# Cross attention, causal attention and eight experts on one core: the experts' step on routed tokens, in slots of 32

## The chip, the cores and the metric

The kernel runs on one core of a Trainium2 chip. The metric is the device time of one execution in microseconds. Three runs of the kernel before gave 585.03, 585.13 and 585.42, median 585.13. The profile shows the instructions of five engines: TensorE (PE, with its weight loads as PEld), VectorE (DVE), ScalarE (ACT), GpSimd (POOL) and SyncE (SP), whose queue issues all DMAs here.

## The reference

The state `x` has 256 tokens of 512 features. Three steps are added to it in turn.

- Cross attention without softmax over a context of 25088 rows: `sigmoid(q k^T / sqrt(128)) v`, with q from the normalized state, and k and v from the context.
- Causal attention with 16 heads of 32 features, low-rank keys and values, a rotary part, and an output projection.
- Eight experts, one for each token, chosen by the largest gate logit:

```
logits = einsum('th,eh->te', xf, gate_w)
onehot = one_hot(argmax(logits), 8)
g = einsum('th,ehd->etd', xf, wg);  u = einsum('th,ehd->etd', xf, wu)
inter  = square(relu(g)) * u * onehot.T[:, :, None]
out    = einsum('etd,edh->th', inter, wd)
```

As written, every expert is computed for every token, and the one-hot vector then clears all but one. An expert has 512 x 128 weights twice (g and u) and 128 x 512 once.

## The kernel before, in words

**Tiles.** The 256 tokens are two tiles of 128 (`tt` or `t`, 0 and 1). The 512 features are four blocks of 128 (`j`, KD = 4). The context is read in 49 chunks of 512 rows.

**Precision.** Where it matters, an f32 operand is split into a high part, rounded by ACT (line 64), and a low part, subtracted on DVE (line 65). `mm3` (lines 67 to 70) then makes three fast matmuls of them (hi x hi, hi x lo, lo x hi) on operands of the type `fp32r`. Other products are plain f32 matmuls, which TensorE runs as two records.

**The loop** (lines 263 to 294). For each chunk: projected keys (`kp_mm`), scores and sigmoid (`scores`), and the product with the context into two PSUM banks, `acc[0]` and `acc[1]`, one for each token tile (`av`, line 192). The products of tile 1 for the last two chunks are put off into the list `late` (eight calls, `AV1`). `prepare` (line 198) takes one piece of a list `todo` per chunk: it loads 128 x 512 weights, splits them and, except for `wv`, stores both halves to DRAM (`spill`). The list has 32 pieces: 4 of `wv`, 16 of `gu` (g and u), 8 of `dn` (down) and 4 of `wo`.

**Behind the loop** (lines 298 to 711) each step is a small function, and the calls at the bottom are its order. `O1`, `O2` and `V` apply the value projection to `acc`. `N1` adds and normalizes: residual add, two steps of moments and a sum on DVE, a power on POOL (line 129), the scaling on DVE (line 134). `X` transposes. `QR`, `CKV`, `KR`, `K`, `VS` and `Q` make queries, keys and values, `S` the scores and exponentials, `PT` their transpose, and `PV` the product with the values: line 457 writes 32 PSUM partitions for each head, so it uses 32 columns of the array. `R1`, `R2` and `AT` divide by the sums, `WO` projects, `N2` normalizes again, `Y` transposes and splits, and `LG` (line 500) takes the logits and writes the one-hot matrix `hot`.

**The experts before.** `GU` multiplies all 128 tokens of a tile by g and u of two experts (512 columns, `mm3`, four blocks: 12 matmuls per pair and tile; the last pair of tile 1 is done expert by expert with 256 columns). `GE` forms relu(g) squared times u times the column of `hot`. `IT` transposes and splits it, `DN` multiplies by the down weights, all experts into one bank `fo`, and `OUT` adds the residual and stores. `load_gu` and `load_dn` fetch the split weights from DRAM behind the loop. `GU` of tile 0 begins while the attention of tile 1 still runs.

**The order.** `in_order` (line 35) ties each instruction of PE, ACT, DVE and POOL to the one before it on its engine, so each engine runs in program order; SP takes its issues in turn. A buffer is named by its tag; with `bufs=2` a new tile waits until all readers of the tile two before it are done. PSUM banks come from one ring of six (`bank`).

Of the kernel before, what the change touches and what calls it, by code (L numbers as in the profile page):

```python
# [20 lines left out]
P = 128  # L21
# [9 lines left out]
LAG = 2  # L31
MASKED = -3.0e38

# [15 lines left out]
def body(ctx, tc, a, out, nch=NCH):  # L49
# [55 lines left out]
    spill = {n: dram.tile([P, 2 * w], F32, name=f"sp_{n}") for n, w in (("wo", KD * D), ("gu", E * 2 * D), ("dn", E * D))}  # L105

    todo = [("wv", at, None, at) for at in range(0, KD * D, D)]
    todo += [("gu", at, 4 * D, at // (4 * D) * 8 * D + at % (4 * D)) for at in range(0, E * 2 * D, D)]
    todo += [("dn", at, D, 2 * at) for at in range(0, E * D, D)]
# [9 lines left out]
    iota8 = sm.tile([P, E], F32, name="iota8")  # L119
    nc.gpsimd.iota(iota8, pattern=[[1, E]], base=-E, channel_multiplier=0, allow_small_or_imprecise_dtypes=True)  # L120
# [176 lines left out]

    x1 = [sb.tile([P, D], F32, name=f"x1{t}") for t in range(2)]
    x2 = [None, None]
# [3 lines left out]
    xn = [None, None]  # L303
# [7 lines left out]

    gu, dn = [None] * E, [None] * E

    def load_gu(e, tag, bufs):
        gu[e] = sb.tile([P, 2, 2 * D], F32R, tag=tag, name=f"gu{e}", bufs=bufs)
        nc.sync.dma_start(f(gu[e]), spill["gu"][:, e * 4 * D:(e + 1) * 4 * D].rearrange("p (i w) -> p i w", i=2))

    def load_dn(e, tag, bufs):
        dn[e] = pair(f"dn{e}", [P, D], tag, bufs)
        for i in range(2):  # L320
            nc.sync.dma_start(f(dn[e][i]), spill["dn"][:, (2 * e + i) * D:(2 * e + i + 1) * D])

    for e, (tag, bufs) in enumerate((("T0", 2), ("T0", 2), ("T1", 1), ("rN", 2), ("rN", 2))):
        load_gu(e, tag, bufs)
    for e, (tag, bufs) in enumerate((("w", 2), ("w", 2), ("kp", 2), ("dn", 1))):
        load_dn(e, tag, bufs)
    trig = sb.tile([64, T], F32, tag="qp0", name="trig")
    nc.sync.dma_start(trig, a["trig"])
    vs = [sb.tile([P, D], F32, tag=f"kp{i}", name=f"vs{i}", bufs=2) for i in range(2)]

    def O1(tt):
        o = tmp(f"o{tt}")
        copy(o, acc[tt])
        return o

    def O2(tt, o):
        split(oh[:, :, toks(tt)], ol[:, :, toks(tt)], transposed(bank(f"o_ps{tt}"), o))

    def V(tt):
        ps = bank(f"v_ps{tt}")  # L340
        for j in range(KD):
            w = slice(j * D, (j + 1) * D)
            mm3(ps, oh[:, j, toks(tt)], ol[:, j, toks(tt)], wv[0][:, w], wv[1][:, w], j == 0, j == KD - 1)
        return ps

    def N1(tt, ps):
        tt2(x1[tt], ps, x_sb[tt], ALU.add)
        xn[tt] = normal(x1[tt], moments(x1[tt], f"b{tt}"), f"xb{tt}")

    def X(tt):  # L350
        copy(xT[tt], transposed(bank(f"xb_ps{tt}"), xn[tt]))
# [12 lines left out]
    ckv, qr = [None] * 2, [None] * 2  # L364

    def CKV(tt):
        ps = bank(f"ckv_ps{tt}")[:, 0:P]
        prod(ps, tt, lambda j: pw["wkvd"][:, toks(j)])
        ckv[tt] = sb.tile([P, P], F32, name=f"ckv{tt}")
        copy(ckv[tt], ps)  # L370

    def QR(tt):
        ps = bank(f"qr_ps{tt}")[0:64, 0:P]
        prod(ps, tt, lambda j: pw["wqr"][:, 64 * j:64 * (j + 1)])
        qr[tt] = sb.tile([32, P], F32, name=f"qr{tt}")
        rotated("q", qr[tt], ps, tt)
        for i, r in enumerate((64, 0)):
            nc.vector.tensor_scalar(qs[r:r + 32, tt, i], qr[tt][:, None, :].broadcast_to([32, KD, P]), 0.125, None, ALU.mult)

    def KR(tt):  # L380
        ps = bank(f"kr_ps{tt}")[0:64, 0:P]
        mm(ps, lhsT=pw["wkr"], rhs=ckv[tt], start=True, stop=True)
        kr = sb.tile([32, P], F32, tag="kr", name=f"kr{tt}")
        rotated("k", kr, ps, tt)
        for r in (64, 0):
            for h in range(2):
                (vcopy if h else copy)(kbd[h][r:r + 32, :, 2 - r // 32:4 - r // 32, toks(tt)],
                                       kr[:, None, None, :].broadcast_to([32, 2, 2, P]))

    def K(tt):  # L390
        for h in range(2):
            ps = bank(f"k_ps{tt}{h}")[:, :2 * P].rearrange("p (g t) -> p g t", g=2)
            for g in range(2):
                mm(ps[:, g, :], lhsT=pw["wku"][:, toks(2 * h + g)], rhs=ckv[tt], start=True, stop=True)
            for j in range(4):
                r = slice(32 * j, 32 * j + 32)
                (vcopy if h else copy)(kbd[h][r, :, j, toks(tt)], ps[r])

    def VS(tt):
        ps = bank(f"vs_ps{tt}")  # L400
        mm(ps, lhsT=ckv[tt], rhs=pw["wvu"], start=True, stop=True)
        copy(vs[tt], ps)

    qps = [None, None]

    def Q(tt, g):
        if g == 0:
            qps[tt] = bank(f"q_ps{tt}").rearrange("p (g t) -> p g t", g=KD)
        prod(qps[tt][:, g, :], tt, lambda j: pw["wq2"][:, j * D + g * P:j * D + (g + 1) * P])
        if g == KD - 1:  # L410
            for i in range(2):
                r = slice(64 * i, 64 * i + 64)
                nc.scalar.activation(qs[r, tt, i], qps[tt][r], AF.Copy, scale=0.125)
# [3 lines left out]
    pr, pt = {}, {}  # L417
# [4 lines left out]
    def S(tt, u):  # L422
        g, h0, n = heads(tt, u)
        nk = P * (tt + 1)
        p3 = bank(f"s{tt}_{u}").rearrange("p (h k) -> p h k", h=n)
# [7 lines left out]
        mx = sm.tile([P, 4], F32, tag="mx", name=f"mx{tt}_{u}", bufs=4)  # L433
        nc.vector.tensor_reduce(mx[:, :n], p3, AX.X, ALU.max, negate=True)
        pr[tt, u] = sb.tile([P, D], F32, tag="wr", name=f"pr{tt}_{u}", bufs=2).rearrange("p (h k) -> p h k", h=n)
        for i in range(n):
            h = 4 * g + h0 + i
            nc.scalar.activation(pr[tt, u][:, i, :], p3[:, i, :], AF.Exp, bias=mx[:, i:i + 1],
                                 accum_out=sums[:, tt, h:h + 1])

    def PT(tt, u):
        n = heads(tt, u)[2]
        ps = bank(f"pt{tt}_{u}")
        for i in range(n):
            for kt in range(tt + 1):
                nc.tensor.transpose(ps[:, toks(i * (tt + 1) + kt)], pr[tt, u][:, i, toks(kt)], ident)  # L446
        pt[tt, u] = sb.tile([P, D], F32, tag="z", name=f"pt{tt}_{u}", bufs=2)
        vcopy(pt[tt, u], ps)

    def PV(tt, u):  # L450
        g, h0, n = heads(tt, u)
        if u == 0:
            pv[tt] = psum.tile([P, KD, P], F32, tag=f"acc{tt}", name=f"pv{tt}")
        for i in range(n):
            r = slice(32 * (h0 + i), 32 * (h0 + i + 1))
            for kt in range(tt + 1):
                mm(pv[tt][r, g, :], lhsT=vs[kt][:, g * P + r.start:g * P + r.stop],  # L457
                   rhs=pt[tt, u][:, toks(i * (tt + 1) + kt)], start=kt == 0, stop=kt == tt)

    rT2, att = [None] * 2, [None] * 2  # L460

    def R1(tt):
# [6 lines left out]
    def R2(tt):  # L469
        ps = transposed(bank(f"r_ps{tt}"), rT2[tt])  # L470
        rT2[tt] = tmp(f"rT{tt}").rearrange("p (g t) -> p g t", g=KD)
        copy(rT2[tt], ps)

    def AT(tt):
        at = tmp(f"at{tt}").rearrange("p (g t) -> p g t", g=KD)
        tt2(at, pv[tt], rT2[tt], ALU.mult)
        att[tt] = [t.rearrange("p (g t) -> p g t", g=KD) for t in pair(f"at{tt}", [P, D], "at")]
        split(*att[tt], at)

    def WO(tt):  # L480
        ps = bank(f"wo_ps{tt}")
        for g in range(KD):
            w = slice(g * D, (g + 1) * D)
            mm3(ps, att[tt][0][:, g, :], att[tt][1][:, g, :], wo[0][:, w], wo[1][:, w], g == 0, g == KD - 1)
        x2[tt] = sb.tile([P, D], F32, tag=f"x{tt}", name=f"x2{tt}")
        tt2(x2[tt], ps, x1[tt], ALU.add)
        xn[tt] = moments(x2[tt], f"c{tt}")

    def N2(tt):
        xn[tt] = normal(x2[tt], xn[tt], f"xc{tt}")  # L490

    def Y(tt):
        ps = transposed(bank(f"xc_ps{tt}"), xn[tt])
        split(yhl[0][:, :, toks(tt)], yhl[1][:, :, toks(tt)], ps)
        yT[tt] = sb.tile([P, KD, P], F32, tag=f"xT{tt}", name=f"yT{tt}")
        copy(yT[tt], ps)

    hot = [None, None]

    def LG(tt):  # L500

        ps = bank(f"lg_ps{tt}")[:, 0:E]
        for j in range(KD):
            mm(ps, lhsT=yT[tt][:, j, :], rhs=pw["gate"][:, j * E:(j + 1) * E], start=j == 0, stop=j == KD - 1)
        lg = sm.tile([P, E], F32, tag="lg", name=f"lg{tt}")
        m1 = sm.tile([P, 1], F32, tag="m1", name=f"m1{tt}")
        vcopy(lg, ps)
        nc.vector.tensor_reduce(m1, lg, AX.X, ALU.max)
        nc.vector.scalar_tensor_tensor(lg, lg, m1, iota8, ALU.is_ge, ALU.mult)
        nc.vector.tensor_reduce(m1, lg, AX.X, ALU.min)  # L510
        hot[tt] = sm.tile([P, E], F32, name=f"hot{tt}")
# [261 lines left out]
```

## Time and profile before

| what | value |
|---|---|
| median of three runs | 585.13 us |
| profiled execution, own time | 584.47 us |
| its span | 582.7 us |
| TensorE busy | 568.9 us, 98% |
| DVE, ACT, POOL busy | 459.9, 395.1, 21.2 us |
| loop's last matmul of `acc[0]` begins | 480.26 us |
| WO(1) ends, first transpose of IT begins | 548.03 us |
| last matmul begins | 578.63 us |
| granted TensorE clock | 1.00 |

A busy TensorE is a modelled figure, since matmuls overlap: a matmul of 512 columns has a duration of about 0.39 us, while the next begins 0.23 us later. So the starts of neighbours count, not the durations. A line number in a row can be that of a helper (lines 64, 65 and 68 to 70 serve many steps); the names of the tiles tell them apart.

### The profile page before, as it was taken

Reading aid. Unit: us, or ns where it says so; the run is one execution under the profiler, and the core shown is the slowest. Engines: PE = TensorE matmul, PEld = TensorE weight load, DVE = VectorE, ACT = ScalarE, POOL = GpSimd, SP = SyncE. Lnnn points to the kernel's source line nnn. Section 1 sums busy time; section 2 is a strip of 40 time slices with the busy share of each in tenths; the row PEclk is TensorE's granted clock in tenths of the full one; section 3 lists DMA queues with packets and bytes.
Section 4 is the critical chain, followed back from the end, with each engine's and each line's share of the span. In section 5 each row is a group of like instructions: output and inputs, shape, how many; then the busy total and the mean of one; then the engine's idle time right before and its main releaser. Section 6 shows DMA issues by size and latency. Waiting matters only on the chain.

```text
span 582.7 us, 7892 instructions
## 1 busy us (share of the span) xinstructions
PE 568.9 (98%) x2952; PEld 476.3 (82%) x2952; DVE 459.9 (79%) x528; ACT 395.1 (68%) x512; POOL 21.2 (4%) x28
## 2 busy tenths in 40 slices
PE   4999999999999999999999999999999998999997
PEld 3888888888888888888888888888888887876886
DVE  6998888888888888888888888787878765667543
ACT  5887777777777777777777776767676753565221
POOL 5200000000000000000000000000000041000000
PEclk9999999999999999999999999999999999999999
DMA  8998787888887888788988897565656477800000
GB/s 293 360 350 299 272 302 271 328 278 321 278 331 269 328 266 336 265 332 288 342 285 307 282 338 242 213 224 209 227 206 232 156 294 260 325 2 1 1 0 38
DMA packets 33527, 144.94 MB, mean 249 GB/s; under 512 B 4241, under 2 KB 4433, under 8 KB 19793
## 3 DMA queue, kind: packets, MB, share of 16 engines
q1 hardware_dynamic: 33488, 144.44, 69.2%
q8 instruction: 23, 0.38, 0.2%
q14 instruction: 16, 0.12, 0.1%
HBM read 129.22 MB, written 15.20 MB: 248 GB/s over the span
## 4 chain that ended last, share of the span: by engine, by line
PE 94%; DVE 3%; DMA 1%; issue 0%; POOL 0%; ACT 0%; SPq 0%; POOLq 0%
PE acc L68 15%; PE acc L69 15%; PE acc L70 15%; PE kp_ps L68 8%; PE kp_ps L69 8%; PE kp_ps L70 8%; PE sc L70 4%; PE sc L69 4%; PE sc L68 4%; PE s L429 2%; PE gu L68 1%; PE gu L70 1%; PE gu L69 1%; PE pt L446 1%; DMA wq_r<-in_wq 1%; PE pv L457 1%
## 5 line engine op out<-in xcount | busy, mean ns | idle before, releaser
L68 PE MATMUL acc<-N,z 128*128 128x512 f32 x392 | 153.9, 393 | 0.0
L69 PE MATMUL acc<-N,z 128*128 128x512 f32 x392 | 153.7, 392 | 0.0
L65 DVE TENSOR_TENSOR N<-rN,N 128x2048 fp32r<-128x2048 f32 (+1 forms) x53 | 112.1, 2119 | 52.2 <-ACT N L64 52.2
L70 PE MATMUL acc<-N,z 128*128 128x512 f32 x392 | 152.5, 389 | 0.0
L65 DVE TENSOR_TENSOR T<-rT,T 128x2048 fp32r<-128x2048 f32 (+1 forms) x49 | 110.2, 2250 | 15.1 <-ACT T L64 15.1
L187 ACT ACTIVATE z<-sc 128x512 f32<-128x512 f32 x98 | 58.7, 599 | 66.4 <-PE sc L70 66.2
L64 ACT CAST N<-rN 128x2048 fp32r<-128x2048 f32 (+1 forms) x55 | 94.4, 1725 | 6.1
L64 ACT CAST T<-rT 128x2048 fp32r<-128x2048 f32 (+1 forms) x55 | 94.4, 1721 | 1.6 <-DMA rT<-in_ctxT 1.5
L70 PEld LDWEIGHTS acc<-N,z 128*128 128x128 f32 x392 | 73.6, 188 | 16.1
L68 PEld LDWEIGHTS acc<-N,z 128*128 128x128 f32 x392 | 74.0, 189 | 12.3
L69 PEld LDWEIGHTS acc<-N,z 128*128 128x128 f32 x392 | 74.0, 189 | 11.6
L68 PE MATMUL kp_ps<-T,wk 128*128 128x512 f32 x196 | 76.9, 392 | 0.0
L70 PE MATMUL kp_ps<-T,wk 128*128 128x512 f32 x196 | 76.5, 390 | 0.0
L69 PE MATMUL kp_ps<-T,wk 128*128 128x512 f32 x192 | 74.7, 389 | 0.0
L189 DVE TENSOR_TENSOR zacc<-zacc,z 128x512 f32<-128x512 f32 x98 | 67.2, 686 | 3.4 <-ACT z L187 1.5
L65 DVE TENSOR_TENSOR z<-z,z 128x512 fp32r<-128x512 f32 x98 | 67.2, 686 | 0.0
L64 ACT CAST z<-z 128x512 fp32r<-128x512 f32 x98 | 61.1, 623 | 3.1
L178 ACT ACTIVATE kp<-kp_ps,bk 128x512 fp32r<-128x512 f32 x49 | 33.8, 691 | 39.7 <-PE kp_ps L70 39.7
L70 PE MATMUL sc<-qp,kp 128*128 128x256 f32 x196 | 55.8, 285 | 0.2 <-DVE kp L179 0.2
L69 PE MATMUL sc<-qp,kp 128*128 128x256 f32 x196 | 55.4, 283 | 0.0
L68 PE MATMUL sc<-qp,kp 128*128 128x256 f32 x196 | 54.9, 280 | 0.0
L68 PEld LDWEIGHTS kp_ps<-T,wk 128*128 128x128 f32 x196 | 37.1, 189 | 7.8
(177 smaller groups left out, 625.9 us busy)
## 6 DMA issues: line engine op xcount, KB each, us to landing
rN<-in_ctxN SPq DMA_DIRECT2D x49, 1024.0 KB, 5.5
rT<-in_ctxT SPq DMA_DIRECT2D x47, 1024.0 KB, 5.7
sp_gu<-w_gu SPq DMA_DIRECT2D x32, 256.0 KB, 4.3
gu<-sp_gu SPq DMA_DIRECT2D x8, 1024.0 KB, 5.6
r_gu<-in_gu SPq DMA_DIRECT2D x16, 256.0 KB, 6.2
sp_dn<-w_dn SPq DMA_DIRECT2D x16, 256.0 KB, 4.4
dn<-sp_dn SPq DMA_DIRECT2D x16, 256.0 KB, 7.0
r_dn<-in_dn SPq DMA_DIRECT2D x8, 256.0 KB, 6.5
```

Source lines behind the costliest of these rows:

```text
L64: copy(hi, src)
L65: eng.tensor_tensor(lo, src, f(hi), ALU.subtract)
L68: mm(ps, lhsT=ahi, rhs=bhi, start=first, stop=False)
L69: mm(ps, lhsT=ahi, rhs=blo, start=False, stop=False)
L70: mm(ps, lhsT=alo, rhs=bhi, start=False, stop=last)
L178: nc.scalar.activation(kp[c][0], ps, AF.Identity, bias=bk)
L187: nc.scalar.activation(z, ps, AF.Sigmoid, scale=1.0 / math.sqrt(128.0))
L189: tt2(zacc, zacc, z, ALU.add)
L429: mm(p3[:, h - h0:h - h0 + 2, :], lhsT=qs[:, tt, h // 2, g, :], rhs=kbd[g // 2][:, g % 2, h:h + 2, :nk], start=tt == 1, stop=tt == 0 and h ...
L446: nc.tensor.transpose(ps[:, toks(i * (tt + 1) + kt)], pr[tt, u][:, i, toks(kt)], ident)
L457: mm(pv[tt][r, g, :], lhsT=vs[kt][:, g * P + r.start:g * P + r.stop], rhs=pt[tt, u][:, toks(i * (tt + 1) + kt)], start=kt == 0, stop=kt == tt)
```

## The change

**The order becomes a table.** The section behind the loop is cut into smaller steps, one engine each as a rule (`Sp` the matmuls of `S`, `Sv` its maximum, `Sa` its exponentials; the letter after a last colon says whether ACT, `a`, or DVE, `v`, copies). A string `ORDER` lists them, and a loop calls them in that order. Attention computes what it did, in another order, and copies are dealt out anew between ACT and DVE. The memset of `qs` now stands directly behind the loop. No expert step stands among the steps of attention any longer: `LGp:0` comes after `WOp:1:3`.

**The experts on their own tokens.** For each token tile there are 11 slots of 32 tokens: slot e for the first 32 tokens of expert e, and three more for experts with more than 32 tokens (a further slot for each 32 of a full expert). Three groups hold 4, 4 and 3 slots.

- `LGv`: `hot` in bf16 and `ids`, the number of the expert less 8. The logits are read from PSUM without a copy.
- `RKp`: two small matmuls of `hot` with a strictly upper triangular matrix and with ones: rank of each token in its expert, and tokens of each expert.
- `RKv`, `RWv`, `RPv`: slots beyond the first by comparison and a running sum; the experts of the three further slots as integers (`which`); and the permutation matrix `perm`, 128 tokens by 384 places.
- `RWs`, `RDs`: SP reads three registers from `which` and loads g, u and down weights of these experts from the inputs, at an address from the register.
- `GAp`, `GAc`: gather by matmul, tokens (high and low part) times `perm`, one matmul each, 384 columns, for each block. `PMp`, `PMc`: `perm` transposed.
- `GUp`: for each slot a plain f32 matmul with 32 columns of weights and 256 moving columns, into 32 PSUM partitions of its own; so are `DNp`'s with 512.
- `DNa`, `DNv`: the result split into high and low part. `SCp`: scatter by matmul with the transposed permutation, into `fo`.

The expert weights are not split any longer: `todo` and `spill` lose `gu` and `dn`, and behind the loop they are loaded once from the inputs, for all eight experts, at half the bytes.

The table from the last steps of attention on, and the core of the diff:

```
...
Sa:1:0 WOp:0:3 PVp:1:5 R1v:1 PVp:1:3 PTc:1:1:a PTp:1:0 N2v:0 R2p:1 PTc:1:0:a PVp:1:1 R2c:1:a PVp:1:0 ATv:1 N2g:0
ATa:1 N2w:0 Ya:0 ATw:1 Yp:0 Yv:0 Yc:0:a WOp:1:0 WOp:1:1 WOp:1:2 WOp:1:3 LGp:0 N2v:1 LGv:0 N2g:1 RKp:0 N2w:1
RKv:0 Yp:1 Ya:1 RWv:0 Yc:1:a RPv:0 RWs:0 LGp:1 Yv:1 PMp:0 GAp:0:0 LGv:1 PMc:0:a GAp:0:1 GAc:0:0:v GAp:0:2
GAc:0:1:a RKp:1 GAp:0:3 GAc:0:2:v GUp:0:0:0 RKv:1 GAc:0:3:a GUp:0:0:1 RWv:1 GUp:0:0:2 RPv:1 RWs:1 GUp:0:0:3
GUp:0:1:0 GEa:0:0 GUp:0:1:1 GEv:0:0 GUp:0:1:2 GUp:0:1:3 GAp:1:2 GEa:0:1 RDs:0 GAp:1:3 GEv:0:1 GAc:1:2:a GAp:1:0
GAc:1:3:a GAp:1:1 GAc:1:0:v ITp:0:1 ITp:0:0 PMp:1 GAc:1:1:a ITc:0:1:v ITc:0:0:v GUp:0:2:0 PMc:1:a GUp:0:2:1
GUp:0:2:2 GUp:0:2:3 DNp:0:0 GEa:0:2 GEv:0:2 GUp:1:1:0 DNa:0:0 RDs:1 GUp:1:1:1 GUp:1:1:2 DNv:0:0 GUp:1:1:3
GUp:1:2:0 GEa:1:1 GUp:1:2:1 GEv:1:1 GUp:1:2:2 GUp:1:2:3 GUp:1:0:0 GEa:1:2 GUp:1:0:1 GEv:1:2 GUp:1:0:2 GUp:1:0:3
DNp:0:1 GEa:1:0 GEv:1:0 ITp:0:2 SCp:0:0:0 DNa:0:1 SCp:0:0:1 ITc:0:2:v ITp:1:0 ITp:1:1 ITp:1:2 DNv:0:1 SCp:0:1:0
ITc:1:0:a ITc:1:2:a DNp:0:2 ITc:1:1:a DNp:1:0 DNa:0:2 DNp:1:1 DNv:0:2 DNa:1:0 DNp:1:2 DNv:1:0 DNa:1:1 SCp:0:1:1
DNa:1:2 DNv:1:1 SCp:0:2:0 SCp:0:2:1 SCp:1:0:0 DNv:1:2 SCp:1:0:1 SCp:1:1:0 SCp:1:1:1 OUv:0 SCp:1:2:0 SCp:1:2:1
OUs:0 OUv:1 OUs:1
```

```diff
 todo = [("wv", at, None, at) for at in range(0, KD * D, D)]
-todo += [("gu", at, 4 * D, at // (4 * D) * 8 * D + at % (4 * D)) for at in range(0, E * 2 * D, D)]
-todo += [("dn", at, D, 2 * at) for at in range(0, E * D, D)]
 todo += [("wo", at, KD * D, at) for at in range(0, KD * D, D)]
...
+    for k, tag in enumerate(("T0", "T0", "rN", "rN")):
+        w = sb.tile([P, 2, 2 * D], F32, tag=tag, name=f"gu{k}", bufs=2)
+        nc.sync.dma_start(w, a["gu"][:, 4 * k * D:4 * (k + 1) * D].rearrange("p (e w) -> p e w", e=2))
...
+    def RKv(tt):
+        full = sm.tile([P, E, 3], F32, tag="full", name=f"full{tt}")
+        count = sm.tile([P, E], F32, tag="count", name=f"count{tt}")
+        tt2(full, rk[tt][:, E:, None].broadcast_to([P, E, 3]), over, ALU.is_gt)
+        nc.vector.tensor_reduce(count, full, AX.X, ALU.add)
+        nc.vector.tensor_tensor_scan(base[tt][:, 1:], one8, count, 0.0, ALU.mult, ALU.add)
...
+        nc.vector.tensor_scalar(perm[tt], place, rb[:, 0:1], u, ALU.subtract, ALU.is_equal)
...
+    def RWs(tt):
+        _, es = nc.values_load_multi_w_load_instructions(
+            ps_["which", tt][0:1, 0:3], engines=(mybir.EngineType.SP,), min_val=0, max_val=E - 1,
...
+        for i in range(3):
+            nc.sync.dma_start(wg[i], a["gu"][:, bass.ds(es[i] * (2 * D), 2 * D)])
...
+    def GAp(tt, j):
+        ps = ps_["yg", tt, j] = bank(f"yg_ps{tt}{j}")[:, :NG * P]
+        for i in range(2):
+            mm(ps, lhsT=yhl[tt][i][:, toks(j)], rhs=perm[tt], start=i == 0, stop=i == 1)
...
+    def GUp(tt, g, j):
+        if j == 0:
+            gps[tt, g] = bank(f"gu{tt}_{g}")[:, :2 * P]
+        for r, at, e in slots(g):
+            w = gu[e] if e < E else more[tt][0][e - E]
+            mm(gps[tt, g][r, :], lhsT=yg[tt][:, j, at], rhs=w[:, 2 * j * P:2 * (j + 1) * P], start=j == 0, stop=j == KD - 1)
...
+    def DNp(tt, g):
+        ps = ps_["dn", tt, g] = bank(f"dn{tt}_{g}")
+        for r, _, e in slots(g):
+            w = dn[e] if e < E else more[tt][1][e - E]
+            mm(ps[r, :], lhsT=ft[:, (NG * tt + g) % 4, r], rhs=w, start=True, stop=True)
...
+    def SCp(tt, g, i):
+        mm(fo[tt], lhsT=permT[tt][rows_of(g), toks(g)], rhs=dps[tt, g][i], start=g == 0 and i == 0, stop=g == NG - 1 and i == 1)
```

## The prediction, on record before the result

> **What bounds the kernel now.** I read the page first (busy times, slices), then the stretches behind the loop, then single instructions in time order. The page, parts 1 and 2:
>
> ```profile
> span 582.7 us, 7892 instructions
> PE 568.9 (98%) x2952; PEld 476.3 (82%) x2952; DVE 459.9 (79%) x528; ACT 395.1 (68%) x512; POOL 21.2 (4%) x28
> PE   4999999999999999999999999999999998999997
> ```
>
> TensorE is busy everywhere but at the start and the end. So removed work counts only if it was TensorE's. The loop stays at one pace while weights are split into high and low parts in it and after they are done (issues of the context loads, two neighbours of each phase):
>
> ```profile
> 257.19 0.33 SPq L149 DMA_DIRECT2D rT<-in_ctxT  x1
> 266.84 0.33 SPq L149 DMA_DIRECT2D rT<-in_ctxT  x1
> ...
> 430.20 0.33 SPq L149 DMA_DIRECT2D rT<-in_ctxT  x1
> 439.84 0.33 SPq L149 DMA_DIRECT2D rT<-in_ctxT  x1
> ```
>
> 9.65 us a chunk with that work, 9.64 without. Behind the loop (stretch, PE, PEld, DVE, ACT, POOL, clock, DMA):
>
> ```profile
> 520.00:540.00 20.00, 20.00 (x134) 12.55 (x133) 14.36 (x25) 10.68 (x37) 0.55 (x1) 1.00 0.00 1
> 540.00:560.00 20.00, 20.00 (x117) 16.45 (x116) 10.95 (x34) 4.63 (x11) 0.55 (x1) 1.00 0.00 1
> 560.00:579.00 19.00, 19.00 (x100) 15.69 (x98) 7.55 (x22) 3.54 (x11) 0.00 (x0) 1.00 0.04 15
> ```
>
> No gap on TensorE, half-idle vector engines, idle DMA: the tail (480 to 579) is TensorE's own work, the experts included. How plain f32 matmuls run, on all columns and on 32 (start, duration, records; each is two records):
>
> ```profile
> 504.13 1.03 PE L429 MATMUL s<-kbd,qs 128*128 128x256 f32 x4
> 504.99 0.38 PE L427 MATMUL s<-mask,identb 128*128 128x512 bf16 x1
> ...
> 511.24 0.32 PE L457 MATMUL pv<-pt,vs 128*32 128x128 f32 x4
> ...
> 519.09 0.65 PE L457 MATMUL pv<-pt,vs 128*32 128x128 f32 x16
> 519.66 0.66 PE L139 MATMUL r_ps<-ident,rx 128*128 128x128 f32 x4
> ```
>
> Two 256-column matmuls take 504.13 to 504.99, 0.43 each; so 128 columns would be 0.213. In the 0.04 us after 511.26 four 32-column matmuls are under way together. Eight of them take 519.09 to 519.66: 0.57 = 2 x 0.213 + 0.14, where one after another would be 1.7. Four run as one; 0.14 is the switch back to full width. Small DVE operations and the end:
>
> ```profile
> 544.42 0.16 DVE L507 COPY lg<-lg_ps 128x8 f32<-128x8 f32 x1
> ...
> 545.41 0.42 DVE L534 SCALAR_TENSOR_TENSOR f<-gu,f 128x256 f32<-128x256 f32 x1
> ...
> 548.23 0.69 DVE L486 TENSOR_TENSOR x<-wo_ps,x 128x512 f32<-128x512 f32 x1 [1.76 <-PE wo_ps L70]
> ...
> 549.97 0.41 DVE L65 TENSOR_TENSOR ft<-it,ft 128x256 fp32r<-128x256 f32 x1
> ...
> 578.63 0.39 PE L70 MATMUL fo<-dn,ft 128*128 128x512 f32 x1
> 579.06 0.69 DVE L555 TENSOR_TENSOR y<-fo,x 128x512 f32<-128x512 f32 x1 [0.81 <-PE fo L70]
> ```
>
> Five small operations take 0.99, so 0.2 each with hand-over; residual add with its moments 1.75 (548.23 to 549.97). The last add ends at 579.75; 2.95 follow (store and close).
>
> **What the Trainium skill says.** "TensorEngine Tiling (Array Packing)", Key Properties: different tiles work in parallel, and "Changing tiling mode (not just tile) drains the TensorE". The trace agrees with both: four at once, 0.14 per switch. "TensorE: Matmul & The Clock Gate", Part 1: an idle window of about 3.4 us halves the clock. The trace has the cold price only at its start (four transposes 1.12 us at 7.38, 0.60 at 552.60) and no cooling after the 1.2 us gap at 489.5. "DMA: Bandwidth & Descriptors", Anatomy of one DMA: some 2.0 us are fixed. This fits here: the two 1 MB moves of `wo` land in 8.5 us (part 6), which leaves 2.1 MB in 6.5, 323 GB/s.
>
> **Part 1, the loop: 0.** 24 of 32 pieces of `prepare` go (a load, a 0.61 cast on ACT, a 0.68 subtraction on DVE, two stores each). The pace above shows they hid under TensorE; were ACT the bound, each would be worth its 0.61. The experts' loads behind the loop shrink from 12 MB to 6 MB: nothing either, since the first use (GUp:0, after 550) is 50 us behind them; late, they would cost what is missing there.
>
> **Part 2, removed from TensorE.** GU: 84 matmuls of 512 columns at 0.23 (starts at 545.98 and 546.21 are 0.23 apart) and 24 of 256 at 0.12: 22.2. DN: 48 x 0.23 = 11.0. IT: 16 x 0.11 = 1.8. Together 35.0. Of it 24 GU matmuls (5.55) and LG(0) (0.79) lie before the end of WO(1), at 548.03.
>
> **Part 3, up to the end of WO(1).** 548.03 - 6.34 = 541.7. Gain at the start, about 1.0: N1's scale for tile 0 took 2.00 at 488.61 beside the memset of `qs` on POOL, which held TensorE 1.2; the memset now comes earlier, and without it the same operation took 0.55 (501.90). POOL's new constants stand before its 0.55 power for N1: 1.8 for `qs`, which waits for AV:3 (about 484.2), and some 1.8 for iotas and memsets (8 columns 0.14, a mask 0.29, 384 columns taken as 0.9), so done near 487.9, when N1 asks near 489. Loss: before WO(1) the chain ATv 0.69, N2w 0.55 and ATa 0.62, ATw 0.69 has only Yp (0.44) to cover it, where GU(0) did: 1.6. For dozens of split copies in a new order, with two score buffers and six PSUM banks, I add 0.8 of waits; the rest is the old work. End of WO(1): 541.7 - 1.0 + 1.6 + 0.8 = 543.1.
>
> **Part 4, routing of tile 0, on TensorE's path.** Counted from there: 0.25 hand-over, N2v:1 1.85 with hand-over, LGv:0 four small 0.8, N2w:1 0.55, RKv three 0.65, RWv three 0.6, RPv six 1.2 and the 384-column comparison 0.45: 6.35. Behind these on DVE stand Yv:1 0.69 and LGv:1 0.8 before the first copy GAc (0.55): GU starts at 8.5. TensorE has LG twice, RK, Yp, PM and GA in that time, about 4; 4.5 are bare. The scan and the value loads have no row; the scan is taken as 0.2 (0.15 to 0.5).
>
> **Part 5, the rest of TensorE's queue.** A group of four slots by one of four blocks: 256 columns, 0.43; a group 1.71; six groups 10.3 (a group of three slots costs the same). DN: 512 columns, 0.853 x 6 = 5.1. GA of tile 1: 8 x 0.174 (384/512 of 0.23) = 1.4. PM:1 0.33, IT 0.66, SC 12 x 0.23 = 2.8; switches 8 x 0.14 = 1.1. Sum 21.7, so the last matmul ends at 30.2 (tile 1's own routing, as long, lies under GUp:0 and is ready at 11.8; GAp:1 comes at 12.0). Then 0.25 + 0.69 + 2.95 = 3.9. OUv:0 stands ahead of the last add on DVE: 0.2. 543.1 + 30.2 + 0.2 + 3.9 = 577.4, against 582.7.
>
> **Part 6, the extra experts' weights.** RWs:0 can be issued when RWv:0 is done, at 4.75. Three moves are 1.57 MB: 2.0 + 4.9 = 6.9. Reading three registers on SP has no row here; from 0 to 4 us, I take 2. They land at 13.7; GUp:0:2 asks at 14.1. For tile 1: 10.2 + 2 + 6.9 = 19.1, asked at 18.4. RDs follow, 0.79 MB each, at 21.6 and 24.1; asked at 24.7 and 27.3. Cost 0.3 to 0.7 at my value, 0 at the low end, some 3.5 at the high one. SP's queue holds nothing else but the final stores. I add 0.4: span 577.8, **4.9 less**. The profiled run was 584.47 for its span of 582.7; the median of the three is 585.13. Predicted median 580.2.
>
> **Rivals.**
> *Weights late* (16%): register reads of 4 us or more, or slower loads; TensorE would stop before GUp:0:2. About 583. For it: less than half a us of slack. Against: DMA is otherwise idle.
> *Cold clock* (9%): TensorE is sparse for 8.5 us; should that count as an idle window, some 2.2 us of the next work run at half pace: 582.4. Against: no bare gap exceeds 2.2.
> *Tiles don't overlap as well* (12%), the case on the slower side: GU and DN one after another are 88 x 0.43 + 22 x 0.853 = 56.6; at four 15.4. Wider moving operands (256, 512 columns, four weights at a time from different places) might run only two at once: 28.3, +12.9: 593. It decides from 20.3 us, an overlap of 2.8. For it: the trace shows 128 columns only. Against: there it is a full four.
> *Denser than thought* (8%): no waits in Part 3 and a shorter routing chain: 577.5.
> That all 11 slots of a tile are computed whatever the tokens are is in the sums already.
>
> **How the numbers follow.** Forecast 55%, its own range 578.3 to 582. Range 577.3 to 584.3: it leaves out the overlap case and a part of the dense one. 0.2% is 1.2 us, about what can be told from no change. Faster: 55 + 8 + 11 (most of the late weights) + 9 = 83%; same 4% (late weights); slower 12 + 1 = 13%.
>
> **What would show it.** The loop's pace 9.64 and its end at 480 unmoved. Records of GUp in fours, 0.43 a block, DNp 0.85 a group. WO(1) ending near 543; about 4.5 us without TensorE work after it, released by DVE. At GUp:0:2 and GUp:1:2 waits on DMA under 1 us. The clock stays at 1.00. The prediction falls if a GUp group takes over 2.5 us, if the first GUp starts over 10 us after WO(1), or if attention loses more than 3 us in its new order.

## The result, and the profile after

The changed kernel took 580.17 us (median of four runs, 579.48 to 580.62) beside 585.27 us for the kernel before (585.03 to 585.62). The ratio is 0.9911, 95% interval 0.9894 to 0.9929. The profiled execution took 580.47 us, its span is 578.5 us. The page of the kernel after, parts 1 and 2:

```profile
span 578.5 us, 7915 instructions
PE 560.4 (97%) x3044; PEld 465.3 (80%) x3044; DVE 447.3 (77%) x513; ACT 388.0 (67%) x497; POOL 22.5 (4%) x36
PE   4999999999999999999999999999999999999697
PEclk9999999999999999999999999999999999999889
```

Two things are new against the page before: a slice at 6 near the end of TensorE's row, and a clock row that no longer holds 9 to the end. The stretches behind the attention of the kernel after (stretch, then the busy time of PE, PEld, DVE, ACT and POOL, the granted clock, the DMA share and GB/s) show both in one place:

```profile
540.00:545.00 5.00, 3.73 (x22) 3.16 (x21) 2.67 (x8) 0.66 (x2) 0.05 (x1) 1.00 0.00 0
545.00:550.00 5.00, 3.29 (x16) 2.83 (x16) 4.02 (x19) 1.20 (x2) 0.50 (x1) 0.59 0.13 22
550.00:555.00 5.00, 5.00 (x49) 3.71 (x51) 3.41 (x17) 1.44 (x3) 0.00 (x0) 0.73 0.78 297
555.00:560.00 5.00, 5.00 (x65) 3.46 (x58) 2.73 (x10) 2.38 (x6) 0.00 (x0) 1.00 0.76 267
```

Between 545 and 550 the granted clock is 0.59, then 0.73, and only then 1.00 again; in the kernel before it was 1.00 there. These are means of a clock that is either 1.00 or 0.50 (see the last section). TensorE's instructions of that stretch in order of time (kernel after; start, duration, then in brackets the idle time and what ended it):

```profile
539.56 0.63 PE L172 MATMUL xc_ps<-ident,xc 128*128 128x128 f32 x4 [1.61 <-DVE xc L167]
542.78 0.95 PE L699 MATMUL lg_ps<-gate,yT 128*128 128x8 f32 x8
545.65 0.17 PE L715 MATMUL rk_ps<-hot,before 128*128 128x8 bf16 x1 [1.92 <-DVE hot L710]
...
546.23 1.09 PE L172 MATMUL xc_ps<-ident,xc 128*128 128x128 f32 x4 [0.38 <-DVE full L723]
547.99 1.88 PE L699 MATMUL lg_ps<-gate,yT 128*128 128x8 f32 x8 [0.68 <-ACT yT L684]
549.72 0.88 PE L788 MATMUL pm_ps<-ident,perm 128*128 128x128 f32 x3
550.25 2.27 PE L775 MATMUL yg_ps<-perm,y 128*128 128x384 f32 x6
...
553.08 1.29 PE L813 MATMUL gu<-gu,yg 128*32 128x256 f32 x20
```

The same four transposes (`xc_ps`) take 0.63 at 539.56 and 1.09 at 546.23; the same eight gate matmuls take 0.95 and then 1.88. WO(1) ends at 542.78, the first expert matmul starts 10.3 us later. All waits of TensorE from there on (kernel after; in total, times, longest):

```profile
PE rk_ps L715 <- DVE hot L710: 1.9, 1, 1.9
PE lg_ps L699 <- ACT yT L684: 0.7, 1, 0.7
PE xc_ps L172 <- DVE full L723: 0.4, 1, 0.4
```

There is no DMA among them. From the first expert matmul to the end TensorE runs without a stop, and the last add starts 1.0 us after OUv:0's:

```profile
573.80 0.68 DVE L865 TENSOR_TENSOR y<-fo,x 128x512 f32<-128x512 f32 x1
...
574.80 0.69 DVE L865 TENSOR_TENSOR y<-fo,x 128x512 f32<-128x512 f32 x1 [0.32 <-PE fo L860]
```

**One scale for all kernels.** The loop does not reach its end at the same time in each execution. Its last score matmul (`sc`) starts at 477.58 in the profile of after, at 478.18 in another profile of the same kernel, and between 477.30 and 478.92 in all kernels of this study, which share the changed kernel's loop. In the one profile of before it starts at 476.94. The executions differ in when TensorE first gets its full clock: by the clock records kept with the traces 12.4 us from the start in the kernel before, 12.8 to 16.6 us in the twelve others, and the start of this matmul comes later by about 0.4 us for each us of that. The kernel before lies 0.2 us below the straight line through the twelve, which scatter by 0.2 us about it themselves, so no loss in the loop beyond that is seen. I count from that matmul (its start is 0; us):

| kernel | WO(1) ends | first GUp | last add starts |
|---|---|---|---|
| before | 71.1 | | 102.1 |
| after | 65.2 | 75.5 | 97.2 |
| after, second profile | 65.2 | 75.3 | 97.5 |
| idle matmuls in the gaps, both profiles | 65.2 | 73.3 | 95.1 |
| spare slots on resident weights | 65.2 | 75.5 | 97.2 |
| no spare slots | 65.2 | 74.2 | 91.2 |
| one column strip | 65.2 | 75.6 | 118.0 |
| old order up to WO(1) | 70.7 | 81.3 | 104.0 |
| the same with idle matmuls | 69.4 | 77.6 | 99.7 |
| routing early | 68.2 | 70.9 | 100.6 |
| routing early, idle matmuls | 66.5 | 69.8 | 98.2 |
| the same, spare group later | 66.5 | 69.8 | 96.0 |

On this scale the change is worth 102.1 - 97.2 = 4.9 us.

### The profile page after: what moved, and what is told of

Read it like the earlier page. It is cut to its first block, busy times and chain, and to the rows that moved or that the text cites. A ratio compares the mean times of both kernels' runs of the same rounds, so it can differ in the third digit from the quotient of the medians.

```text
span 578.5 us, 7915 instructions
## 1 busy us (share of the span) xinstructions
PE 560.4 (97%) x3044; PEld 465.3 (80%) x3044; DVE 447.3 (77%) x513; ACT 388.0 (67%) x497; POOL 22.5 (4%) x36
## 4 chain that ended last, share of the span: by engine, by line
PE 94%; DVE 3%; issue 1%; ACT 1%; DMA 1%; POOL 0%; SPq 0%; DVEq 0%; ACTq 0%; POOLq 0%
PE acc L98 15%; PE acc L99 15%; PE acc L100 15%; PE kp_ps L99 8%; PE kp_ps L98 8%; PE kp_ps L100 8%; PE sc L100 4%; PE sc L99 4%; PE sc L98 4%; PE s L576 2%; PE gu L813 2%; PE q_ps L479 1%; PE pt L600 1%; PE dn L842 1%; PE pv L615 1%
```

## The experiments

### Does the cold clock cost, and how much?

Idle matmuls (512 columns, into a PSUM bank that nobody reads until the scatter) keep TensorE busy in the gaps of the routing: seven behind LGp:0, one behind RKp:0, two ahead of LGp:1, one behind it.

```diff
+    def WM(n):
+        for _ in range(n):
+            if not junk:
+                junk[0] = psum.tile([P, D], F32, tag="acc0", name="junk")
+            mm(junk[0], lhsT=wo[0][:, 0:P], rhs=wo[0][:, 0:D], start=True, stop=True)
...
-LGp:0 N2v:1 LGv:0 N2g:1 RKp:0 N2w:1
+LGp:0 WM:7 N2v:1 LGv:0 N2g:1 RKp:0 WM:1 N2w:1
```

> The changed kernel with eleven idle matmuls of 512 columns (0.23 us each) put where TensorE waits for the routing: 7 before RKp:0, 1 before Yp:1, 2 before LGp:1, 1 behind it. Cold-clock theory: TensorE loses its full clock in the routing and runs Yp:1, LGp:1, PMp:0 and GAp:0 at half pace; the granted clock then stays at 1.00 between 545 and 555, Yp:1 takes 0.6 instead of 1.1, LGp:1 0.9 instead of 1.9, and the first GUp begins 2.0 us earlier; time 1.2 to 2.5 us below the changed kernel (577.7 to 579.0). Rival, that DVE's chain is simply longer than I worked out: less than 0.3 us, and the first GUp where it was.

Measured: 578.83 us, ratio to before 0.9890 (0.9875 to 0.9904). The stretches of this kernel:

```profile
545.00:550.00 5.00, 4.56 (x26) 3.08 (x25) 4.48 (x22) 1.20 (x2) 0.55 (x1) 1.00 0.00 0
550.00:555.00 5.00, 5.00 (x73) 3.38 (x77) 4.51 (x22) 1.72 (x4) 0.00 (x0) 1.00 0.91 311
```

and its instructions that answer to those above:

```profile
547.26 0.63 PE L171 MATMUL xc_ps<-ident,xc 128*128 128x128 f32 x4
...
548.56 1.06 PE L698 MATMUL lg_ps<-gate,yT 128*128 128x8 f32 x8 [0.21 <-ACT yT L683]
...
549.92 0.52 PE L787 MATMUL pm_ps<-ident,perm 128*128 128x128 f32 x3
550.19 1.30 PE L774 MATMUL yg_ps<-perm,y 128*128 128x384 f32 x6
...
551.93 3.66 PE L812 MATMUL gu<-gu,yg 128*32 128x256 f32 x64
```

The clock stays at 1.00, transposes take 0.63 again, PM 0.52 for 0.88, GA 1.30 for 2.27. The first GUp comes 8.1 us after WO(1) instead of 10.3. The work was added to, and the time fell. The theory holds. The same kernel was run once more beside the changed kernel itself:

> The changed kernel with eleven idle matmuls in the routing's gaps once more, beside the changed kernel itself. Theory (cold clock costs 1.2 us or more): 1.2 to 2.0 us below the changed kernel. Rival: within 0.6 us of it.

> The changed kernel itself, for the comparison on one chip: 579.8 to 581.0 us, with the clock's drop at 545 to 555.

Measured: 578.33 us (577.64 to 579.48, ratio to before 0.9880, 0.9863 to 0.9897) against 580.83 us (579.58 to 581.40, ratio 0.9916, 0.9903 to 0.9930). That is 2.5 us, which is what the scale says too: 97.5 - 95.1 = 2.4, and 2.1 against the first profile of after. The clock agrees over whole executions: the mean granted is 0.999 or 1.000 in all eight runs of the changed kernel with idle matmuls, and 0.991 to 0.993 in eight of the nine without them; the ninth, at 0.997, is the fastest of them, 579.48 us. It is more than was expected for the pair at most (2.0). The kernel with idle matmuls is faster than both the kernel before and the changed one.

### Do the late weights cost?

The three spare slots of a tile use weights that are already there; the register reads and the six late loads of a tile are left out, so tokens in spare slots meet a wrong expert.

```diff
-            w = gu[e] if e < E else more[tt][0][e - E]
+            w = gu[e % E]
...
-            w = dn[e] if e < E else more[tt][1][e - E]
+            w = dn[e % E]
```

> The three further slots multiply with the weights of experts 0 to 2, which are already there, so the register reads on SP and all twelve late loads are gone; tokens in further slots so get wrong weights. If the loads are hidden: within 0.4 us of the changed kernel. If they hold back GUp:0:2 or GUp:1:2 behind a wait that the trace puts down to another engine: 1 to 3 us less.

Measured: 580.36 us, ratio 0.9923 (0.9908 to 0.9938), all three marks on the scale as in the changed kernel. The loads cost nothing. SP's queue in the kernel after shows why:

```profile
548.32 0.89 SPq L761 DMA_DIRECT2D mg<-in_gu  x2
549.38 0.33 SPq L761 DMA_DIRECT2D mh<-in_gu  x1
555.13 0.85 SPq L761 DMA_DIRECT2D mg<-in_gu  x2
```

`which` is written at 547.18, so the register reads and the start of the issue take 1.1 us. The moves land 4.0 (`mg`) and 5.4 us (`mh`) after their issue, so the last near 554.8; GUp:0:2 asks at 558.8. For tile 1 the margin is smaller: the last lands near 561.6, and GUp:1:2 asks at 563.1.

### Do four strips run at once?

The first block of a group stays on four strips of 32 columns; blocks 1 to 3 go to one strip for all slots, so the sums are of other things, with as many matmuls of the same shape.

```diff
+            o = r if j == 0 else slice(0, SL)
-            mm(gps[tt, g][r, :], lhsT=yg[tt][:, j, at], rhs=w[:, 2 * j * P:2 * (j + 1) * P], ...
+            mm(gps[tt, g][o, :], lhsT=yg[tt][:, j, at], rhs=w[:, 2 * j * P:2 * (j + 1) * P], ...
```

> GUp's blocks 1 to 3 of all slots of a group go to the same 32 columns of the array (sums of several slots are mixed there), block 0 as before; the same number of matmuls. If the gain comes from four strips running together: the three blocks take 3 x 0.43 x 22 = 28.4 us instead of 7.7, so 19 to 21 us slower than the changed kernel (599 to 601). If 32-column matmuls are cheap by themselves: within 3 us of it.

Measured: 601.34 us (one run), 118.0 on the scale, 20.8 later than the changed kernel. Two groups of gate and up in this kernel:

```profile
553.23 11.41 PE L815 MATMUL gu<-gu,yg 128*32 128x256 f32 x64
```

With 4 strips the same 64 records took 3.66. One after another they would be 2 x (0.43 + 12 x 0.43) = 11.2. So matmuls on one strip follow each other at 0.43 and those on four strips share one such time, at 256 columns as at 128. The Trainium skill, "TensorEngine Tiling (Array Packing)", Key Properties, has different tiles work in parallel; this pair of runs agrees, with 0.45 for a pack of four. The gain of the change rests on it. On one strip the four also write the same PSUM partitions; which of the two makes them follow each other is not parted here.

### What is the order by the table worth?

The steps up to WO(1) stand in the order of the kernel before, with the expert steps taken out, the copies on the engines that they had, and the memset of `qs`, with the new constants of POOL, back in its old place. From LGp:0 on the table is unchanged.

```diff
-EXa ZSv ZSp O1:0:a AV:0 ZRv O2p:0 AV:1 O2a:0 AV:2 O2v:0 AV:3 Vp:0:0 Vp:0:1 Vp:0:2 Vp:0:3 AV:4 N1v:0 AV:5 AV:6
...
+O1:0:a ZSv ZSp ZRv O2p:0 O2a:0 O2v:0 EXa AV:0 AV:1 Vp:0:0 Vp:0:1 Vp:0:2 Vp:0:3 N1v:0 N1g:0 N1w:0 AV:2 AV:3 AV:4
...
+PTp:1:6 PTc:1:6:v PVp:1:5 PTp:1:7 PTc:1:7:v R1v:1 PVp:1:6 PVp:1:7 R2p:1 R2c:1:a ATv:1 ATa:1 ATw:1 WOp:1:0 ...
```

> The changed kernel with the steps up to WO(1) in the order of the kernel before, its engines for the copies too, the experts' steps as in the changed kernel. My sum: the old order without expert matmuls among it lays bare the chains of tile 1 (PT, its copy, PV, and AT before WO), so its section is 1.5 to 4 us longer than the table's: 581.7 to 584. Rival, that the order is worth nothing: within 0.6 us of the changed kernel.

Measured: 587.26 us (583.29 to 588.15), ratio 1.0023 (1.0007 to 1.0038). Without the table the change is no gain at all, at the clock that this kernel gets: its eleven executions reach from 583.29 us, at a mean clock of 0.997, to 588.15 at 0.988. The median is above both expectations. The longest waits up to WO(1) of this kernel (in total, times, longest), and then its stretches:

```profile
PE wo_ps L97 <- ACT at L649: 2.1, 1, 2.1
...
PE xb_ps L171 <- DVE xb L166: 1.4, 2, 1.2
PE pv L619 <- DVE pt L609: 1.2, 2, 1.0
```

```profile
545.00:550.00 5.00, 5.00 (x20) 4.06 (x20) 1.05 (x2) 0.00 (x0) 0.00 (x0) 0.69 0.00 0
550.00:555.00 5.00, 2.03 (x11) 1.51 (x9) 4.45 (x22) 1.20 (x2) 0.55 (x1) 0.65 0.02 5
555.00:560.00 5.00, 5.00 (x23) 4.14 (x27) 3.02 (x12) 1.17 (x3) 0.00 (x0) 0.50 0.86 301
```

Nothing covers the 2.1 us in which tile 1's attention is divided, rounded and split ahead of WO(1), where before GU(0) ran. And the clock falls earlier, at WO(1), and stays down longer. To part the two, idle matmuls were put into the gaps ahead of WO(1) and into those of the routing:

> The kernel with the steps up to WO(1) in the order of before, plus idle matmuls in the two gaps ahead of WO(1) and in the gaps of the routing. Theory (its loss of 7 us against the changed kernel is partly the cold clock that starts at WO(1)): 580.5 to 583.5 us, the spacing of WO(1)'s matmuls 0.23 us instead of 0.43. Rival (the exposed waits alone make it): only the 1.3 us that the warm routing is worth, 585 to 586.5.

Measured: 582.61 us (581.69 to 584.36), ratio 0.9960 (0.9948 to 0.9971), inside what the theory said. WO(1)'s matmuls in this kernel follow at 0.23 (546.97, 547.20, 547.43), where without the idle ones they had 0.43:

```profile
546.97 0.39 PE L97 MATMUL wo_ps<-wo,at 128*128 128x512 f32 x1
547.20 0.39 PE L98 MATMUL wo_ps<-wo,at 128*128 128x512 f32 x1
547.43 0.40 PE L99 MATMUL wo_ps<-wo,at 128*128 128x512 f32 x1
```

On the scale the clock made 70.7 - 69.4 = 1.3 up to WO(1) and 2.5 between WO(1) and the first GUp. What is left, 69.4 against 65.2, is the order itself, with the engines of the copies and the place of the memset: 4.2 us with a warm clock. With another 0.3 (`o_ps`) the waits make 5.0 in the old order, against 2.6 in the table's (listed below, Part 3), so 2.4 of the 4.2; where the rest lies was not settled. No run has the table with the experts of before, so what the table would give there is not known.

### Can the routing be hidden?

Tile 0's gate goes in front of the second matmul group of WO(1), its ranks in front of the last, and tile 1's norm behind tile 0's permutation:

```diff
-WOp:1:0 WOp:1:1 WOp:1:2 WOp:1:3 LGp:0 N2v:1 LGv:0 N2g:1 RKp:0 N2w:1
-RKv:0 Yp:1 Ya:1 RWv:0 Yc:1:a RPv:0 RWs:0 LGp:1 ...
+WOp:1:0 LGp:0 LGv:0 WOp:1:1 WOp:1:2 RKp:0 WOp:1:3 RKv:0 RPv:0 RWv:0 RWs:0 N2v:1 N2g:1
+GAp:0:0 GAp:0:1 ... GUp:0:0:0 N2w:1 GUp:0:0:1 GUp:0:0:2 GUp:0:0:3 Yp:1 Ya:1 ...
```

> The gate of the first token tile is moved in front of the second matmul group of WO(1), the ranks in front of its last, and tile 1's norm behind tile 0's permutation, so that tile 0's routing on VectorE runs under WO(1). Theory (the routing is a chain between WO(1) and the first expert matmul, and each us of it moves the end): the first gate-and-up matmul comes 3 to 5.5 us after WO(1) instead of 10.3, tile 1's routing lies under tile 0's experts, and the time is 575.0 to 578.0 us. Rival (tile 1's routing, which now starts later, is what the end follows): TensorE gets the same idle time further on, and the time is 579 to 582.

> The kernel with the routing moved early, and six idle matmuls ahead of the token gather, so that no gap is bare. Theory (the clock falls there too): another 0.5 to 1.5 us less than with the routing early alone, and a granted clock of 1.00 in all stretches from 540 to 560. Rival (with the routing under WO(1) TensorE is busy enough): within 0.3 us of it.

Measured: 581.55 us (ratio 0.9944, 0.9925 to 0.9963) without and 581.76 us (0.9945, 0.9925 to 0.9965) with six idle matmuls. The first GUp does come 4.6 us earlier than in the changed kernel, and the end comes later: the rival of the first. Idle matmuls did not change the median: the second rival. In the profile without them the clock is down at WO(1) (0.69 between 540 and 545), but that execution, 583.75 us, is the odd one of its four; the other three have 0.998 to 1.000. With the gate and ranks between its groups TensorE is mostly busy enough. The two longest waits of TensorE in the version with idle matmuls, from 540 on:

```profile
PE gu L812 <- DMA mh<-in_gu: 2.2, 1, 2.2
PE xc_ps L171 <- DVE xc L166: 1.6, 1, 1.6
```

Tile 1's routing now starts later, its weights are asked for at 556.94, and its spare group, second in its line of groups, waits 2.2 us for them. So tile 1's first group and one down group were put ahead of the spare group:

```diff
-GUp:1:2:0 GEa:1:1 GUp:1:2:1 GEv:1:1 GUp:1:2:2 GUp:1:2:3 GUp:1:0:0 GEa:1:2 GUp:1:0:1 GEv:1:2 GUp:1:0:2 GUp:1:0:3
-DNp:0:1 GEa:1:0 GEv:1:0 ITp:0:2 SCp:0:0:0 DNa:0:1 SCp:0:0:1 ITc:0:2:v
+GEa:1:1 GUp:1:0:0 GEv:1:1 GUp:1:0:1 GUp:1:0:2 GUp:1:0:3 DNp:0:1 GEa:1:0 GEv:1:0 ITp:0:2 SCp:0:0:0 DNa:0:1 ITc:0:2:v
+GUp:1:2:0 GUp:1:2:1 GUp:1:2:2 GUp:1:2:3 GEa:1:2 GEv:1:2 SCp:0:0:1
```

> The kernel with the routing early and idle matmuls, with tile 1's first group and a down group put ahead of its spare group, to fill the stretch in which TensorE waited for tile 1's late weights. Theory (that wait of some 3 us is what the early routing lost): TensorE waits for no DMA, and the time is 577.5 to 579.0 us, 3 less than before this edit. Rival (the loss is the dense stretch itself, which now holds tile 1's transposes and gate): 580.5 to 582.

Measured: 579.41 us (578.84 to 580.38), ratio 0.9897 (0.9882 to 0.9913). The wait on the DMA is gone; what remains in the tail (543 to 578):

```profile
PE it L830 <- DVE f L824: 0.5, 1, 0.5
PE yg_ps L774 <- DVE perm L749: 0.3, 1, 0.3
PE yg_ps L774 <- DVE le L732: 0.3, 1, 0.3
```

On the scale the edit gave 2.2 us (98.2 - 96.0) of the 3 it was meant to give, and the time lies 0.4 above the range of the theory, well below that of the rival. Still it isn't better than the idle matmuls alone (578.33 in the same comparison). From the first GUp to the last add it takes 26.2 us, where those take 21.8: tile 1's transposes (0.66 us), its gate (1.06), the permutation's transpose (0.49), the waits above and the switches around them now stand in the dense part. In the changed kernel they stood in the routing's gap, which is to say that the gap was not empty.

### What do the spare slots cost?

The third group of each tile, the late weights and the search for full experts are left out; tokens beyond 32 of an expert get nothing.

```diff
-NG = 3
+NG = 2
...
-                for i in range(4) if 4 * g + i < E + 3]
+                for i in range(4) if 4 * g + i < E]
```

> Leaves the spare slots out: no third group of three blocks, no late weights, no search for the experts that overflow, so rows beyond 32 of an expert are not computed. Theory (the tail is TensorE's sum): per tile a gate-and-up group of 1.71 less a quarter, a down group of 0.6, a transpose, two scatter matmuls of 0.23 and a third of the gather go, some 3.5 to 4, and 0.5 of VectorE's chain, so 571.5 to 574.0 us. Rival (the spare groups only fill what would be waits for tile 1's routing): 576 to 579.

Measured: 575.25 us (574.72 to 576.17), ratio 0.9843 (0.9822 to 0.9863): between the two expectations. The first GUp comes 9.0 after WO(1), 1.3 earlier than with spare slots, and the rest is 4.7 shorter, 17.0 for 21.7. It would be more, but here the stretch at half clock, 547.0 to 553.9, reached into the experts (the clock is 0.62 between 550 and 555), and the first two groups, 3.66 us in the changed kernel, took

```profile
552.01 4.54 PE L809 MATMUL gu<-gu,yg 128*32 128x256 f32 x64
```

Without that 0.9 the profiled execution (574.72 us) would stand within the theory's range, the median a little above it. So the spare slots are mostly TensorE's sum, as the theory has it, and cost some 6 us on the scale, more than the whole gain of the change.

## Why the prediction was right, point by point

**The time** was forecast at 580.2 and came at 580.17; the span at 577.8 and came at 578.5. The sum is good to 0.7 us because its terms were wrong in both directions, and the median is closer still because the profiled execution lay 0.3 above its median, where the one before had lain 0.7 below. Both are luck: a loss of 1.8 us that the forecast took as nothing was mostly made good by three terms that had been taken too dear.

**Part 1, the loop: right.** The loop keeps its 9.64 us a chunk. What its end differs by is no more than what executions differ by.

**Part 2, removed work: not tested by itself.** The 35.0 us are in the sum only.

**Part 3, the end of WO(1): a little too late.** Predicted 71.1 - 6.3 - 1.0 + 1.6 + 0.8 = 66.2 on the scale, measured 65.2. The gap ahead of the transposes is the predicted one to the digit, 1.61. All waits of TensorE from the loop's end to WO(1) (kernel after):

```profile
PE xc_ps L172 <- DVE xc L167: 1.6, 1, 1.6
PE xb_ps L172 <- DVE xb L167: 0.4, 1, 0.4
PE k_ps L534 <- ACT ckv L498: 0.4, 1, 0.4
PE ckv_ps L479 <- ACT xT L474: 0.2, 1, 0.2
```

0.6 of new small waits where 0.8 were added, and the wait for N1 fell from 1.2 to 0.4, as the moved memset said (N1's scale for tile 0, 2.00 us in the kernel before, takes 0.55). So the waits grew by 0.9, from 1.7 (1.4 for `xb` and 0.3 for `o_ps` in the kernel before), where 1.4 had been foreseen; another 0.45 of the difference lies in no wait and was not located. What the prediction did not see is how much the table does: it takes the experts' cover as replaced at 2.4 us of waits, and the run with the old order shows that without the table the section is 4.2 us longer with a warm clock and 5.5 with its own.

**Part 4, the routing: the step that failed.** "GU starts at 8.5" holds for a TensorE at full clock: 8.1 with the idle matmuls. But the sum took the clock as 1.00, and it came to 10.3, and to 10.1 in the second profile. A first GUp over 10 us after WO(1) was one of the prediction's own signs of being wrong, and a clock that stays at 1.00 one of its signs of being right: on both it failed here, though its total held. The rival "cold clock", at 9%, is what happened, with the size given to it: 2.2 us, 10.3 - 8.1; its 582.4 did not come because other terms were smaller. Bare were 3.0 us of the gap (1.9, 0.7 and 0.4), where 4.5 had been computed; TensorE's own work in it, most of it at half clock, took 7.3, where about 4 had been. The reason against it, that no bare gap exceeds 2.2, was true (the longest is 1.92) and decided nothing.

Before those 1.92 stood another 1.61 and between 542.78 and 545.65 only 0.95 of gate matmuls. The Trainium skill, "TensorE: Matmul & The Clock Gate", Part 1, speaks of an idle window of about 3.4 us; read as one unbroken gap, as the prediction read it, this trace does not agree. The last section shows how far it does when the window is read as a fixed stretch of time. On DVE the steps took what they were priced at: `perm` was ready 5.96 after WO(1), 6.35 had been computed, and the scan, taken at 0.2, took 0.18.

**Part 5, the rest of the queue: right.** 21.7 predicted, 21.7 measured (553.08 to 574.76). A pack of four matmuls of gate and up was 0.45 for 0.43. The rival "tiles don't overlap" had its price right too: shut to one strip for three blocks of four, it costs 20.8.

**Part 6, the extra weights: too dear by 0.4.** `which` was ready 4.4 after WO(1), not 4.75; the register reads took 1.1, not 2; the three loads took 6.5 from the first issue, 6.9 had been estimated; and the late start of GUp moved the need from 14.1 to 16.0. They landed at 12.0: 4 us of slack, 1.6 for tile 1, and no cost. The fixed 2.0 us in the estimate are not shown here: the section that the prediction names in the Trainium skill, "DMA: Bandwidth & Descriptors", Anatomy of one DMA, is about transfers that GpSimd issues, here SP issues them, and the 323 GB/s were worked out with the 2.0, so the 8.5 us of `wo` confirm neither.

**The end** was 0.4 shorter than taken: OUv:0 did not hold up the last add.

On the span: -0.3 (start 0.6 later, section 1.0 shorter), +1.8, 0, -0.4, -0.4: +0.7.

## What to carry to other kernels

Where a chain on a vector engine takes the place of dense matmuls, price TensorE's sparse work twice, at full and at half clock, and don't rule the second out because each single gap is short: what went with a fall here was little work within 3.4 us (last section). Idle matmuls in the gaps decide it in one run. Work taken off TensorE pays only as far as the waits it covered find other cover: here 35.0 us less work gave 4.9, since 10.3 of routing (which holds the gate and tile 1's transposes that were there before) and 21.7 of gather, experts and scatter took its place. To move a chain earlier is worth less than its gap, if the gap holds work that must then be done elsewhere.

## What was not expected of the hardware

- The clock fell with no idle time over 1.92 us, and not at the same instruction each time. In the second profile of the changed kernel tile 1's transposes still took 0.63 and only the gate behind them 1.88; in the one cold execution with the routing early it was down before WO(1) was done, after a single gap of 1.61 us and a gate of 8-column matmuls.
- It changes at fixed instants, and to 1.00 or 0.50, never between. In all thirteen traces each change comes a whole number of stretches of 3.413 us after the first full clock. The stretch before the fall, and the two at half clock (first the kernel after, then its second profile; columns as above):

```profile
542.45:545.86 3.41, 1.48 (x13) 1.23 (x11) 2.67 (x9) 0.00 (x0) 0.55 (x1) 1.00 0.00 0
545.86:552.69 6.83, 5.79 (x24) 5.11 (x25) 4.61 (x21) 2.16 (x4) 0.00 (x0) 0.50 0.49 164
...
544.35:547.76 3.41, 0.82 (x6) 0.52 (x5) 3.06 (x15) 0.90 (x2) 0.55 (x1) 1.00 0.02 5
547.76:554.59 6.83, 6.48 (x33) 5.22 (x37) 5.04 (x24) 1.74 (x4) 0.00 (x0) 0.50 0.65 229
```

- This fits what the Trainium skill says of the window in "TensorE: Matmul & The Clock Gate", Part 1: it is 3413 ns long and runs free of the kernel, so that the same kernel changes its clock at different instructions.
- What went before a fall was little work in one such stretch, not one long gap. The traces have 394 whole stretches at full clock from 470 us on. In nine of them TensorE was busy for at most 1.60 us, with the 8-column matmuls of gate and ranks not counted, and after each of the nine came half clock; in the others it was busy for 1.75 us or more, and the clock stayed. (Busy time is the profile's, so modelled.) With the 8-column matmuls counted the two kinds do not part: one stretch of 2.50 us was followed by half clock. The rule was read off afterwards, and no run was made to test it.
- One wait of 2.0 us for a DMA in an otherwise dense stretch went with a clock of 0.66 between 565 and 570; a wait of 2.2 us at the same place, in the version with idle matmuls 15 us earlier, left it at 1.00. The first lies in one stretch, 562.40 to 565.81, with TensorE busy for 1.46 us; the second is divided at 564.30, and the stretch up to there has 1.75.
- From `which` on DVE to the first issue on SP, three register reads included, took 1.1 us for tile 0.
